# A decoder layer with routed experts: experts add straight into the output, and a branch for rare steps moves to the middle

## The chip, the cores and the metric

The kernel runs on one core of one Trainium2 chip. The metric is the device time of a whole execution in microseconds: the median of three runs, and beside it one execution that the hardware profiler recorded, with all instructions, waits and DMA packets. Engines are TensorE (PE; PEld are its weight loads), VectorE (DVE), ScalarE (ACT), GpSimd (POOL) and SyncE (SP, which only issues transfers).

## The reference

Eight rows of 256 tokens with 256 features pass three blocks with residuals: a linear attention, a cross attention to a context, and a mixture of eight experts of which each token takes its best two.

```python
x = x + _L0_attn_ref(_layernorm(x), ...)
x = x + _L0_xattn_ref(_layernorm(x), ctx_1024, ctx_1024, ...)
x = x + _L0_ffn_ref(_layernorm(x), ...)      # itself returns its input plus the experts' sum
...
combine, idx = _top2_gate(xn, Wg)
for each expert e:                            # W1[e]: 256 x 1024, W2[e]: 1024 x 256
    h = gelu(xn @ W1[e] + b1[e])
    out += gate[e] * (h @ W2[e] + b2[e])      # gate is 0 for tokens that did not choose e
```

Everything is float32.

## The kernel before

**Front.** For each of the eight rows the attention, the cross attention and the gate are computed; the loops of the rows overlap. `last_norms` writes the normed tokens to a DRAM tensor `rows_d`, `base` writes the residual part of the result to a DRAM tensor `acc` (L609). Each token's two choices get a slot each in a DRAM table `slots` (token number and gate), sorted by expert in tiles of 128; unused slots keep token numbers from NTOK = 2048 up, for which `rows_d` has rows of zeros and `acc` has spare rows.

**Expert steps.** The tokens of one tile are worked on by one expert in one step. At most NSTEP = 39 steps can be needed; how many are is known only on the chip (`total`). SURE = NSTEP - 3 = 36 steps are always run. For step s, `said` loads the expert or the tile number from a list in SBUF into a register of an engine; then

- `fetch_slots` (SP) loads token numbers and gates of the tile, `fetch_weights` (SP) the expert's first weight matrix (w1, 1 MB, three buffers, two steps ahead) and second bias (b2, three buffers);
- `gather` (POOL, indirect DMA, three steps ahead) fetches the 128 token rows, `turn` transposes them on PE, and DVE copies them out of PSUM (L889);
- `first_chunk` (L906, L910): in eight chunks PE multiplies by w1 into PSUM tiles `ph`, and ACT applies the gelu; `second_chunk` (L919) multiplies the chunks of the step before by the second matrix, which stays in SBUF, into `py`. First and second chunks of neighbouring steps alternate on PE;
- `add_out` (DVE, L934) makes yg = gate * py + bias, and `scatter` (POOL, L940) adds its rows to `acc` by an accumulating indirect DMA. Each scatter waits until the one before has landed.

`steps` is a generator with the order of all this for steps first to last; the orders of PE, ACT, DVE and SP are those of the source, and `in_turn` keeps POOL's.

**End.** After the 36 steps all five engines load `total`, and `tc.If(n_steps > SURE)` (L1212, L1216) holds the three rare steps. Behind it SP copies `acc` to the output (L1225). In the arm that is not taken each engine waits for its own last instruction (SP and POOL for their transfers) and then adds to the semaphores what the skipped instructions would have added.

Of the kernel before, what the change touches and what calls it, by code (L numbers as in the profile page):

```python
# [23 lines left out]
CLAMPED = "the list is made on the chip and clamped to this range"  # L24
# [5 lines left out]
def decoder_kernel(  # L30
# [57 lines left out]
    slots = dram.tile([NTILE, 2 * P], I32, name="slots")  # L88
    slot_rows = slots[:, :].rearrange("q (r c) -> (q r) c", c=2)
    rows_d = dram.tile([NTOK + P, D], F32, name="rows_d")  # L90
    acc = dram.tile([NTOK + P, D], F32, name="acc")

    def ps(name):
        return psum.tile([P, 512], F32, tag="ps", name=name)

    def wide(name):
        return psum.tile([P, 512], F32, tag="wide", name=name)
# [4 lines left out]
    def tokens(t, b):  # L102

        return t[S * b : S * (b + 1), :].rearrange("(s p) d -> p s d", p=P)
# [149 lines left out]
    vcols = const("vcols", [P, n_rows])  # L254
    gamma_c = vcols[:, n_b1 : n_b1 + KD]
# [596 lines left out]
    plans, ids, xgs, w1s, b2s, ready, hidden, summed = ({} for _ in range(8))  # L852

    def fetch_slots(s):
        q_sp = said(s, 1, ET.SP)
        ids[s] = mpool.tile([P, 2], I32, tag="ids", name=f"ids{s}", bufs=16)
        got = nc.sync.dma_start(ids[s], slot_rows[bass.ds(q_sp * P, P), :])
        if s in (0, NA):
            for name in puts[0 : RA * T * 2] if s == 0 else puts:
                tc.add_manual_dep(got.ins, name, WRITTEN, reason="all slots are written")  # L860

    def fetch_weights(s):
        e_sp = said(s, 0, ET.SP)
        w1s[s] = mpool.tile([P, KD, F], F32, tag="w1", name=f"w1_{s}", bufs=3)
        nc.sync.dma_start(
            w1s[s], w1_rows[bass.ds(e_sp * D, D), :].rearrange("(k p) f -> p k f", p=P)
        )
        b2s[s] = mpool.tile([P, D], F32, tag="b2", name=f"b2_{s}", bufs=3)
        nc.sync.dma_start(b2s[s], b2_flat[bass.ds(e_sp * D, D)].partition_broadcast(P))

    def reach(s):

        return RA * S if s < NA else NTOK + P
# [6 lines left out]
        ))  # L880

    def turn(s):
        p = ps(f"pt_{s}")
        xg = xgs.pop(s)
        for k in range(KD):
            nc.tensor.transpose(p[:, k * P : (k + 1) * P], xg[:, k * P : (k + 1) * P], ident)  # L886
        ready[s] = mpool.tile([P, KD, P], F32, tag="xgT", name=f"xgT{s}")
# [7 lines left out]
    CHUNKS = [c for pair in zip(range(FC // 2), range(FC // 2, FC)) for c in pair]  # L895

    def first_chunk(s, c):
        if c == CHUNKS[0]:
            hT = mpool.tile([P, FC, P], F32, tag="hT", name=f"hT{s}")
            p = [wide(f"ph_{s}_{i}").rearrange("p (c n) -> p c n", n=P) for i in range(2)]  # L900
            hidden[s] = hT, p, said(s, 0, ET.Activation)
        hT, p, e_act = hidden[s]
        half, at = divmod(c, FC // 2)
        p = p[half][:, at, :]
        for k in range(KD):
            nc.tensor.matmul(  # L906
                p, w1s[s][:, k, c * P : (c + 1) * P], ready[s][:, k, :],
                start=(k == 0), stop=(k == KD - 1),
            )
        nc.scalar.activation(  # L910
            hT[:, c, :], p, AF.Gelu_apprx_tanh,
            bias=vcols[:, bass.ds(e_act * FC + c, 1)],
        )

    def second_chunk(s, c):
        if c == CHUNKS[0]:
            summed[s] = ps(f"py_{s}"), said(s, 0, ET.PE)
        p, e_pe = summed[s]
        nc.tensor.matmul(  # L919
            p[:, 0:D], hidden[s][0][:, c, :], w2_flat[:, bass.ds((e_pe * FC + c) * D, D)],  # L920
            start=(c == CHUNKS[0]), stop=(c == CHUNKS[-1]),
        )

    def gate_of(s):
        return ids[s][:, 1:2].bitcast(F32)
# [1 line left out]
    def scale_bias(s):  # L927
        nc.scalar.activation(b2s[s], b2s[s], AF.Copy, scale=gate_of(s))  # L928

    def add_out(s):  # L930
        p, _ = summed.pop(s)
        del hidden[s]
        yg = mpool.tile([P, D], F32, tag="yg", name=f"yg{s}", bufs=3)
        nc.vector.scalar_tensor_tensor(  # L934
            yg, p[:, 0:D], gate_of(s), b2s.pop(s), op0=ALU.mult, op1=ALU.add
        )
        in_time(scatter, s, yg)

    def scatter(s, yg):
        in_turn(nc.gpsimd.indirect_dma_start(  # L940
            out=acc[0 : reach(s), :],
            out_offset=bass.IndirectOffsetOnAxis(ap=ids.pop(s)[:, 0:1], axis=0),
            in_=yg[:, :], in_offset=None, compute_op=ALU.add,
        ))

    held, holding = [], [False]
# [1 line left out]
    def in_time(what, *args):  # L948
        if holding[0]:
            held.append((what, args))  # L950
        else:
            what(*args)
# [4 lines left out]
            what(*args)  # L957
        held.clear()

    SURE = NSTEP - 3  # L960
    SLOTS, ROWS, WEIGHTS = 5, 3, 2

    def steps(first, last):


        got = max(NA, first + ROWS)
        for s in range(first, last + 1):
            if s + WEIGHTS < last and s > first:
                fetch_weights(s + WEIGHTS)
            while 6 <= s and got <= min(s + SLOTS, last - 1):  # L970
                fetch_slots(got)
                got += 1
            if s + ROWS < last:
                in_time(gather, s + ROWS)
            at = 0
            for j, c in enumerate(CHUNKS):
                took = 0.0
                if s < last:
                    first_chunk(s, c)
                    took += 0.44  # L980

                for c in CHUNKS[at : at + (2 if s == last - 1 else 1)]:
                    if s > first:
                        second_chunk(s - 1, c)
                        took += 0.43
                    at += 1
                if s > first and j == 1:
                    scale_bias(s - 1)
                if s > first and at == FC:
                    at += 1  # L990
                    add_out(s - 1)
                if j == FC - 3 and s + 1 < last:
# [5 lines left out]
            yield took  # L998

    work = steps(0, SURE)  # L1000

# [207 lines left out]
    for _ in plan:  # L1209
        pass  # L1210
    meanwhile(1e6)
    n_steps = nc.values_load(  # L1212
        total[0:1, 0:1], min_val=0, max_val=NSTEP,
        skip_runtime_bounds_check_because=CLAMPED,
    )
    with tc.If(n_steps > SURE):  # L1216
# [8 lines left out]
    nc.sync.dma_start(out.rearrange("b s d -> (b s) d"), acc[0:NTOK, :])  # L1225

# [1 line left out]
_A, _X, _F = "L0_attn_", "L0_xattn_", "L0_ffn_"  # L1228
_INS = [
# [31 lines left out]
```

## Time and profile before

| | us |
|---|---|
| median of 3 runs | 456.35 (455.56 to 458.42) |
| profiled execution | 453.33 |
| its span, first to last instruction | 451.6 |
| PE busy | 432.7 (96%) |
| ACT, DVE, POOL busy | 212.6, 186.4, 186.9 |
| scatters: time on POOL, issue to landing (median) | 1.59 each, 5.8 |
| gathers: time on POOL | 1.00 each |

The span is what the page and all answers of the trace count from; the 1.7 us between it and the execution's time lie around it. In the page's strips each digit is the busy share of one fortieth of the span in tenths (11.3 us). A wait line names who waited, for whom, the total in us, how often, and the longest. An indirect DMA's time on POOL is the making of its descriptors; its landing comes later. Rows of the trace that end in q (PEldq, SPq) are the sequencer of an engine: waits, register work, branches and DMA issues.

### The profile page before, as it was taken

Reading aid. Unit: us, or ns where it says so; the run is one execution under the profiler, and the core shown is the slowest. Engines: PE = TensorE matmul, PEld = TensorE weight load, DVE = VectorE, ACT = ScalarE, POOL = GpSimd, SP = SyncE. Lnnn points to the kernel's source line nnn. Section 1 sums busy time; section 2 is a strip of 40 time slices with the busy share of each in tenths; the row PEclk is TensorE's granted clock in tenths of the full one; section 3 lists DMA queues with packets and bytes.
Section 4 is the critical chain, followed back from the end, with each engine's and each line's share of the span. In section 5 each row is a group of like instructions: output and inputs, shape, how many; then the busy total and the mean of one; then the engine's idle time right before and its main releaser. Section 6 shows DMA issues by size and latency. Waiting matters only on the chain. (4 is left out here: it accounts for less than half of the span.)

```text
span 451.6 us, 8531 instructions
## 1 busy us (share of the span) xinstructions
PE 432.7 (96%) x2679; PEld 373.6 (83%) x2679; DVE 186.4 (41%) x692; ACT 212.6 (47%) x551; POOL 186.9 (41%) x201
## 2 busy tenths in 40 slices
PE   9999999999999999999999999999999999999960
PEld 7568777776868689999999999999999999999950
DVE  2676878687898767454111112121111212121100
ACT  3644555564555455454444444444444444444420
POOL 7314363636445662637243342424333242432220
PEclk9999999999999999999999999999999999999995
DMA  8703266755603254797776857577675766757225
GB/s 227 218 25 117 71 210 64 217 115 174 132 23 114 42 176 140 203 222 181 198 225 182 235 154 239 160 232 204 188 222 168 220 187 221 195 195 219 47 31 195
DMA packets 48369, 74.38 MB, mean 165 GB/s; under 512 B 9773, under 2 KB 37810, under 8 KB 48290
## 3 DMA queue, kind: packets, MB, share of 16 engines
q1 hardware_dynamic: 39298, 63.10, 46.3%
q0 software_dynamic: 8208, 9.91, 12.4%
q10 hardware_dynamic: 816, 0.79, 0.6%
q8 instruction: 24, 0.39, 0.4%
q14 instruction: 23, 0.19, 0.2%
HBM read 64.44 MB, written 11.44 MB: 168 GB/s over the span
## 5 line engine op out<-in xcount | busy, mean ns | idle before, releaser
L906 PEld LDWEIGHTS ph<-xgT,w 128*128 128x128 f32 x1152 | 169.5, 191 | 13.2 <-ACT hT L910 0.7
L906 PE MATMUL ph<-xgT,w 128*128 128x128 f32 x1152 | 174.8, 275 | 0.6 <-ACT hT L910 0.3
L919 PE MATMUL py<-w_s,hT 128*128 x576 | 170.3, 381 | 0.0
L910 ACT ACTIVATE hT<-ph,vcols 128x128 f32<-128x128 f32 x288 | 105.3, 367 | 137.2 <-PE ph L906 133.1
L940 POOL DMA_INDIRECT acc<-yg,ids x36 | 57.1, 1587 | 138.3 <-DMA acc<-yg,ids 75.9
L889 DVE TENSOR_SCALAR xgT<-pt,vcols 128x128 f32<-128x128 f32 x72 | 26.2, 405 | 151.9 <-PE pt L886 151.9
L919 PEld LDWEIGHTS py<-w_s,hT 128*128 128x128 f32 x576 | 88.3, 192 | 0.6
L877 POOL DMA_INDIRECT xg<-rows_d,ids x36 | 36.0, 1000 | 18.5 <-PE ph L906 10.7
L934 DVE SCALAR_TENSOR_TENSOR yg<-py,ids,b 128x256 f32<-128x256 f32 x36 | 17.4, 483 | 44.9 <-ACT hT L910 33.9
L733 POOL DMA_INDIRECT slots<-pay,posi x32 | 31.8, 993 | 9.0 <-issue 8.0
L347 PE MATMUL pxkv<-xwkv_s,cT 128*128 128x512 f32 x64 | 30.1, 593 | 0.0
L347 PE MATMUL pkv<-wkv_s,hT 128*128 128x512 f32 x64 | 29.9, 593 | 0.0
L347 PEld LDWEIGHTS pxkv<-xwkv_s,cT 128*128 128x128 f32 x64 | 11.5, 190 | 8.0 <-issue 7.7
L928 ACT ACTIVATE b<-b,ids 128x256 f32<-128x256 f32 x36 | 17.9, 498 | 0.0
L347 PEld LDWEIGHTS pkv<-wkv_s,hT 128*128 128x128 f32 x64 | 11.1, 190 | 8.2 <-issue 8.1
L309 POOL TENSOR_TENSOR rs_b<-ve_b,mhalf 128x2 f32<-128x2 f32 x8 | 8.2, 1022 | 23.1 <-DVE ve_b L322 23.1
L309 POOL TENSOR_TENSOR rs_a<-ve_a,mhalf 128x2 f32<-128x2 f32 x8 | 5.7, 708 | 26.9 <-DVE ve_a L322 25.9
L347 PEld LDWEIGHTS po<-wo_s,turnedoT 128*128 128x128 f32 x64 | 12.1, 190 | 4.6 <-issue 3.3
L511 ACT COPY turnedoT<-pto 128x512 f32<-128x512 f32 x8 | 4.7, 585 | 23.6 <-PE pto L341 23.6
L410 PE MATMUL pq<-hT,wq_s 128*128 128x256 f32 x64 | 15.2, 381 | 0.2 <-ACT hT L386 0.2
L347 PE MATMUL pfc<-xwfc_s,turnedq2T 128*128 128x256 f32 x64 | 15.2, 380 | 0.0
L347 PE MATMUL po<-wo_s,turnedoT 128*128 128x256 f32 x64 | 15.2, 380 | 0.0
(193 smaller groups left out, 523.4 us busy)
## 6 DMA issues: line engine op xcount, KB each, us to landing
w<-in_L_ffn_W_dram SPq DMA_DIRECT2D x36, 1024.0 KB, 5.4
w_s<-in_L_ffn_W_dram SPq DMA_DIRECT2D x8, 1024.0 KB, 8.6
b<-in_L_ffn_b_dram SPq DMA_DIRECT2D x36, 128.0 KB, 3.1
x<-in_x_dram SPq DMA_DIRECT2D x8, 256.0 KB, 3.5
rows_d<-h SPq DMA_DIRECT2D x8, 256.0 KB, 6.3
acc<-x SPq DMA_DIRECT2D x8, 256.0 KB, 5.2
c<-in_ctx_dram SPq DMA_DIRECT2D x7, 256.0 KB, 3.0
ids<-slots SPq DMA_DIRECT2D x36, 1.0 KB, 2.2
```

Source lines behind the costliest of these rows:

```text
L309: in_turn(nc.gpsimd.tensor_tensor(dst, src, mhalf[:, 0:n], ALU.pow))
L347: nc.tensor.matmul(p[:, 0:width], srcT[:, k, t * P : (t + 1) * P], w[:, k, 0:width], start=(k == 0), stop=(k == KD - 1),)
L410: nc.tensor.matmul(p[:, m, :], wq_s[:, k, m * P : (m + 1) * P], st["hT"][:, k, :], start=(k == 0), stop=(k == KD - 1),)
L733: ins = nc.gpsimd.indirect_dma_start(out=slot_rows, out_offset=bass.IndirectOffsetOnAxis(ap=posi[:, t, c : c + 1], axis=0), in_=pay[:, at ...
L877: in_turn(nc.gpsimd.indirect_dma_start(out=xgs[s][:, :], out_offset=None, in_=rows_d[0 : reach(s), :], in_offset=bass.IndirectOffsetOnAxis ...
L889: nc.vector.tensor_scalar(ready[s][:, k, :], p[:, k * P : (k + 1) * P], gamma_c[:, k : k + 1], beta_c[:, k : k + 1], op0=ALU.mult, op1=ALU ...
L906: nc.tensor.matmul(p, w1s[s][:, k, c * P : (c + 1) * P], ready[s][:, k, :], start=(k == 0), stop=(k == KD - 1),)
L910: nc.scalar.activation(hT[:, c, :], p, AF.Gelu_apprx_tanh, bias=vcols[:, bass.ds(e_act * FC + c, 1)],)
L919: nc.tensor.matmul(p[:, 0:D], hidden[s][0][:, c, :], w2_flat[:, bass.ds((e_pe * FC + c) * D, D)], start=(c == CHUNKS[0]), stop=(c == CHUNK ...
L928: nc.scalar.activation(b2s[s], b2s[s], AF.Copy, scale=gate_of(s))
L934: nc.vector.scalar_tensor_tensor(yg, p[:, 0:D], gate_of(s), b2s.pop(s), op0=ALU.mult, op1=ALU.add)
L940: in_turn(nc.gpsimd.indirect_dma_start(out=acc[0 : reach(s), :], out_offset=bass.IndirectOffsetOnAxis(ap=ids.pop(s)[:, 0:1], axis=0), in_= ...
```

## The change

`acc` is gone: `base` writes to the output, the scatters add into it, and the copy at the end is left out. A scatter now carries a bound: rows with a token number beyond it are dropped instead of being added to spare rows.

The branch for the three rare steps no longer stands at the end but in step FORK = SURE - 18 = 18, ahead of its seventh chunk, and has PE, DVE, ACT and SP alone. What it runs, `seldom`, uses tiles that are free by then (attention weights and the like) in place of new buffers. Its gathers are issued in steps 15 to 17 and its slot loads in steps 14 to 16, whether needed or not; its scatters are issued in any case in steps 19, 24 and 29 ahead of the fifth chunk (`late` tiles hold what they add; where the steps are not needed all their rows are beyond the bound). `ids` has 24 buffers instead of 16, `b2` four instead of three.

```diff
-    acc = dram.tile([NTOK + P, D], F32, name="acc")
+    out_rows = out.rearrange("b s d -> (b s) d")
...
-        nc.sync.dma_start(acc[NTOK:, :], zero)
...
-        nc.sync.dma_start(tokens(acc, b), x3)
+        nc.sync.dma_start(tokens(out_rows, b), x3)
...
     def fetch_weights(s):
         e_sp = said(s, 0, ET.SP)
-        w1s[s] = mpool.tile([P, KD, F], F32, tag="w1", name=f"w1_{s}", bufs=3)
...
+        b2s[s] = bo_b
+        if s < SURE:
+            w1s[s] = mpool.tile([P, KD, F], F32, tag="w1", name=f"w1_{s}", bufs=3)
+            b2s[s] = mpool.tile([P, D], F32, tag="b2", name=f"b2_{s}", bufs=4)
...
+    lent = {}
+
+    def own(kind, s, make):
+        if s < SURE:
+            return make()
+        if kind not in lent:
+            lent[kind] = make()
+        return lent[kind]
...
     def turn(s):
-        p = ps(f"pt_{s}")
+        p = own("pt", s, lambda: ps(f"pt_{s}"))
...
+    def add_out(s):
+        sum_out(s)
+        in_time(scatter, s)
+
+    def scatter(s):
         in_turn(nc.gpsimd.indirect_dma_start(
-            out=acc[0 : reach(s), :],
+            out=out_rows[0 : min(reach(s), NTOK), :],
             out_offset=bass.IndirectOffsetOnAxis(ap=ids.pop(s)[:, 0:1], axis=0),
-            in_=yg[:, :], in_offset=None, compute_op=ALU.add,
+            in_=ygs.pop(s), in_offset=None, compute_op=ALU.add,
+            bounds_check=min(reach(s), NTOK) - 1, oob_is_err=False,
         ))
...
-    SURE = NSTEP - 3
+    SURE = NSTEP - RARE
+    FORK = SURE - 18
...
+            rare = SURE + s - FORK
+            if SURE <= rare + 4 < NSTEP:
+                fetch_slots(rare + 4)
+            if SURE <= rare + 3 < NSTEP:
+                gather(rare + 3)
             at = 0
             for j, c in enumerate(CHUNKS):
+                if s == FORK and j == 6:
+                    seldom()
+                rare, behind_fork = divmod(s - FORK - 1, 5)
+                if j == 4 and 0 <= rare < RARE and behind_fork == 0:
+                    scatter(SURE + rare)
...
+    def seldom():
+        n_steps = nc.values_load(
+            total[0:1, 0:1], engines=[ET.PE, ET.DVE, ET.Activation, ET.SP],
+            min_val=0, max_val=NSTEP, skip_runtime_bounds_check_because=CLAMPED,
+        )
+        with tc.If(n_steps > SURE):
+            for s in range(SURE, NSTEP):
+                ygs[s] = late[s - SURE]
+            for s in range(SURE, NSTEP):
+                fetch_weights(s)
+                turn(s)
+                scale_bias(s)
+                for c in CHUNKS:
+                    first_chunk(s, c)
+                for c in CHUNKS:
+                    second_chunk(s, c)
+                sum_out(s)
...
-    n_steps = nc.values_load(
-        total[0:1, 0:1], min_val=0, max_val=NSTEP,
-        skip_runtime_bounds_check_because=CLAMPED,
-    )
-    with tc.If(n_steps > SURE):
-        for s in range(SURE, NSTEP):
-            fetch_slots(s)
-            fetch_weights(s)
-        for s in range(SURE, NSTEP):
-            gather(s)
-        turn(SURE)
-        for _ in steps(SURE, NSTEP):
-            pass
-    nc.sync.dma_start(out.rearrange("b s d -> (b s) d"), acc[0:NTOK, :])
```

More of the change, by code (lines that the diff above doesn't have):

```diff
@@ L851, in decoder_kernel @@
     done = []
-    plans, ids, xgs, w1s, b2s, ready, hidden, summed = ({} for _ in range(8))
+    plans, ids, xgs, w1s, b2s, ready, hidden, summed, ygs = ({} for _ in range(9))
     def fetch_slots(s):
         q_sp = said(s, 1, ET.SP)
-        ids[s] = mpool.tile([P, 2], I32, tag="ids", name=f"ids{s}", bufs=16)
+        ids[s] = mpool.tile([P, 2], I32, tag="ids", name=f"ids{s}", bufs=24)
         got = nc.sync.dma_start(ids[s], slot_rows[bass.ds(q_sp * P, P), :])
@@ L863, in fetch_weights, with first_weights @@
         e_sp = said(s, 0, ET.SP)
-        w1s[s] = mpool.tile([P, KD, F], F32, tag="w1", name=f"w1_{s}", bufs=3)
-        nc.sync.dma_start(
-            w1s[s], w1_rows[bass.ds(e_sp * D, D), :].rearrange("(k p) f -> p k f", p=P)
-        )
-        b2s[s] = mpool.tile([P, D], F32, tag="b2", name=f"b2_{s}", bufs=3)
-        nc.sync.dma_start(b2s[s], b2_flat[bass.ds(e_sp * D, D)].partition_broadcast(P))
+        b2s[s] = bo_b
+        if s < SURE:
+            w1s[s] = mpool.tile([P, KD, F], F32, tag="w1", name=f"w1_{s}", bufs=3)
+            b2s[s] = mpool.tile([P, D], F32, tag="b2", name=f"b2_{s}", bufs=4)
+        w = w1_rows[bass.ds(e_sp * D, D), :].rearrange("(k p) f -> p k f", p=P)
+        if s < SURE:
+            nc.sync.dma_start(w1s[s], w)
+        else:
+            w1s[s] = wkv_s, xwkv_s
+            for i, half in enumerate(w1s[s]):
+                at = i * (F // 2)
+                nc.sync.dma_start(half[:, :, 0 : F // 2], w[:, :, at : at + F // 2])
+        nc.sync.dma_start(b2s[s], b2_flat[bass.ds(e_sp * D, D)].partition_broadcast(P))
+    def first_weights(s, k, c):
+        if s < SURE:
+            return w1s[s][:, k, c * P : (c + 1) * P]
+        half, at = divmod(c, FC // 2)
+        return w1s[s][half][:, k, at * P : (at + 1) * P]
+    lent = {}
+    def own(kind, s, make):
+        if s < SURE:
+            return make()
+        if kind not in lent:
+            lent[kind] = make()
+        return lent[kind]
     def reach(s):
@@ L886, in turn @@
             nc.tensor.transpose(p[:, k * P : (k + 1) * P], xg[:, k * P : (k + 1) * P], ident)
-        ready[s] = mpool.tile([P, KD, P], F32, tag="xgT", name=f"xgT{s}")
+        ready[s] = bv_b.rearrange("p (k q) -> p k q", k=KD)
+        if s < SURE:
+            ready[s] = mpool.tile([P, KD, P], F32, tag="xgT", name=f"xgT{s}")
         for k in range(KD):
@@ L895, in decoder_kernel, with hidden_tiles @@
     CHUNKS = [c for pair in zip(range(FC // 2), range(FC // 2, FC)) for c in pair]
+    def hidden_tiles(s):
+        if s < SURE:
+            hT = mpool.tile([P, FC, P], F32, tag="hT", name=f"hT{s}")
+            return [hT[:, c, :] for c in range(FC)]
+        pair = [ft("x", f"hT{s}{i}", [P, FC // 2, P], bufs=4) for i in range(2)]
+        return [pair[c // (FC // 2)][:, c % (FC // 2), :] for c in range(FC)]
     def first_chunk(s, c):
         if c == CHUNKS[0]:
-            hT = mpool.tile([P, FC, P], F32, tag="hT", name=f"hT{s}")
-            p = [wide(f"ph_{s}_{i}").rearrange("p (c n) -> p c n", n=P) for i in range(2)]
+            hT = own("hT", s, lambda: hidden_tiles(s))
+            p = own("ph", s, lambda: [
+                wide(f"ph_{s}_{i}").rearrange("p (c n) -> p c n", n=P) for i in range(2)
+            ])
             hidden[s] = hT, p, said(s, 0, ET.Activation)
@@ L906, in first_chunk @@
             nc.tensor.matmul(
-                p, w1s[s][:, k, c * P : (c + 1) * P], ready[s][:, k, :],
+                p, first_weights(s, k, c), ready[s][:, k, :],
                 start=(k == 0), stop=(k == KD - 1),
@@ L910, in first_chunk @@
         nc.scalar.activation(
-            hT[:, c, :], p, AF.Gelu_apprx_tanh,
+            hT[c], p, AF.Gelu_apprx_tanh,
             bias=vcols[:, bass.ds(e_act * FC + c, 1)],
@@ L916, in second_chunk @@
         if c == CHUNKS[0]:
-            summed[s] = ps(f"py_{s}"), said(s, 0, ET.PE)
+            summed[s] = own("py", s, lambda: ps(f"py_{s}")), said(s, 0, ET.PE)
         p, e_pe = summed[s]
         nc.tensor.matmul(
-            p[:, 0:D], hidden[s][0][:, c, :], w2_flat[:, bass.ds((e_pe * FC + c) * D, D)],
+            p[:, 0:D], hidden[s][0][c], w2_flat[:, bass.ds((e_pe * FC + c) * D, D)],
             start=(c == CHUNKS[0]), stop=(c == CHUNKS[-1]),
@@ L928, in scale_bias, with sum_out @@
         nc.scalar.activation(b2s[s], b2s[s], AF.Copy, scale=gate_of(s))
-    def add_out(s):
+    RARE = 3
+    late = [w[:, k, 0:D] for w in (wo_s, xwq_s) for k in range(KD)]
+    def sum_out(s):
         p, _ = summed.pop(s)
         del hidden[s]
-        yg = mpool.tile([P, D], F32, tag="yg", name=f"yg{s}", bufs=3)
+        ygs[s] = late[s - SURE] if s >= SURE else mpool.tile(
+            [P, D], F32, tag="yg", name=f"yg{s}", bufs=3
+        )
         nc.vector.scalar_tensor_tensor(
-            yg, p[:, 0:D], gate_of(s), b2s.pop(s), op0=ALU.mult, op1=ALU.add
+            ygs[s], p[:, 0:D], gate_of(s), b2s.pop(s), op0=ALU.mult, op1=ALU.add
         )
-        in_time(scatter, s, yg)
-    def scatter(s, yg):
+    def add_out(s):
+        sum_out(s)
+        in_time(scatter, s)
+    def scatter(s):
         in_turn(nc.gpsimd.indirect_dma_start(
-            out=acc[0 : reach(s), :],
+            out=out_rows[0 : min(reach(s), NTOK), :],
             out_offset=bass.IndirectOffsetOnAxis(ap=ids.pop(s)[:, 0:1], axis=0),
-            in_=yg[:, :], in_offset=None, compute_op=ALU.add,
+            in_=ygs.pop(s), in_offset=None, compute_op=ALU.add,
+            bounds_check=min(reach(s), NTOK) - 1, oob_is_err=False,
         ))
@@ L998, in steps @@
             yield took
+    def seldom():
+        n_steps = nc.values_load(
+            total[0:1, 0:1], engines=[ET.PE, ET.DVE, ET.Activation, ET.SP],
+            min_val=0, max_val=NSTEP, skip_runtime_bounds_check_because=CLAMPED,
+        )
+        with tc.If(n_steps > SURE):
[10 more added lines that the diff above has]
+                sum_out(s)
     work = steps(0, SURE)
@@ L1211, in decoder_kernel @@
     meanwhile(1e6)
-    n_steps = nc.values_load(
-        total[0:1, 0:1], min_val=0, max_val=NSTEP,
-        skip_runtime_bounds_check_because=CLAMPED,
-    )
-    with tc.If(n_steps > SURE):
-        for s in range(SURE, NSTEP):
-            fetch_slots(s)
-            fetch_weights(s)
-        for s in range(SURE, NSTEP):
-            gather(s)
-        turn(SURE)
-        for _ in steps(SURE, NSTEP):
-            pass
-    nc.sync.dma_start(out.rearrange("b s d -> (b s) d"), acc[0:NTOK, :])
 _A, _X, _F = "L0_attn_", "L0_xattn_", "L0_ffn_"
```

## The prediction

> **What bounds the kernel now.** I read the span in forty slices, then the timeline of the last fifteen microseconds, then busy time by stretch.
>
> ```profile
> PE   9999999999999999999999999999999999999960
> ...
> PEclk9999999999999999999999999999999999999995
> ```
>
> TensorE is the bound to within two slices of the end. Busy time by stretch (per engine: us and count; then granted clock, DMA share, GB/s):
>
> ```profile
> core 0: us, PE busy (x) PEld busy (x) DVE busy (x) ACT busy (x) POOL busy (x), PEclk, DMA share, GB/s
> 300.00:360.00 60.00, 60.00 (x417) 56.17 (x416) 10.42 (x26) 27.39 (x74) 20.61 (x16) 1.00 0.69 201
> ...
> 436.90:441.60 4.70, 0.00 (x0) 0.00 (x0) 0.48 (x1) 0.00 (x0) 1.55 (x1) 0.87 0.28 31
> 441.60:451.60 10.00, 0.00 (x0) 0.00 (x0) 0.00 (x0) 0.00 (x0) 0.00 (x0) 0.50 0.57 211
> ```
>
> In the expert steps PE is busy 60.00 of 60.00 us; one step is 7.25 us (the yg instructions on DVE stand at 302.88 and 310.12). Nothing off PE can gain time there. The tail is different (start, us, engine, what, idle time before it and who ended that):
>
> ```profile
> 435.79 1.03 PE L919 MATMUL py<-w_s,hT 128*128 x4
> ...
> 436.91 0.48 DVE L934 SCALAR_TENSOR_TENSOR yg<-py,ids,b 128x256 f32<-128x256 f32 x1 [4.75 <-PE py L919]
> 437.67 1.55 POOL L940 DMA_INDIRECT acc<-yg,ids  x1 [3.69 <-DVE yg L934]
> 441.56 0.61 SPq L1225 DMA_DIRECT2D out_dram<-acc  x1
> ```
>
> PE ends at 435.79 + 1.03 = 436.82. The last scatter goes at 437.67, lands 3.8 us later (the median that the DMA view gives for this stretch), and only then SP starts the copy of acc to the output, which lands after 8.3 us. From PE's end to the span's end are 14.8 us in which no engine computes anything but that one sum.
>
> **The copy goes: a gain.** Without acc, the base rows and the scatters write the output itself, so L1225 and its wait vanish. What stays after the last landing (SP goes on at 441.56) is the program's end. SP's trace there shows one semaphore instruction each 0.06 us: six of them and two drains took 0.43 us after the copy landed (449.85 to 450.28), and the closing barrier 1.28 us (450.28 to 451.56). Now up to ten waits are left behind the last scatter, 0.6 us. New end: 441.56 + 0.6 + 1.28 = 443.4, 8.2 us before the old one. A 128 KB write of zeros into acc (L252, at 16.2 us, DMA alone) goes too, worth nothing under a full PE.
>
> **The branch moves into step 18: a loss on PE.** Before, the branch at the end cost nothing: PE's and ACT's lay under the tail, SP's 20 us earlier. Its rows (minimum/median/maximum ns):
>
> ```profile
> L1216 ACTq COMPARE_BRANCH  x1: 45/45/45, 433.8 to 433.8; - x1
> L1216 PEldq COMPARE_BRANCH  x1: 3477/3477/3477, 434.5 to 434.5; - x1
> L1216 DVEq COMPARE_BRANCH  x1: 72/72/72, 437.6 to 437.6; - x1
> ...
> L1216 POOLq INC_SWDGE_SEM  x1: 1584/1584/1584, 438.5 to 438.5; - x1
> ```
>
> Now PE, DVE, ACT and SP each load the step count and jump over three steps of code after chunk 5 of step 18, and in the other arm each waits for all it has issued and adds the skipped counts. On PE, matmuls of the old trace at this place lie end to end; its sequencer issues the two transposes of step 19 about 1.6 us before PE has run them (the register work ahead of the next chunk's matmul leads it by 1.1 to 1.35 us). The load is 0.31 us and the branch begins some 1.2 us before PE runs dry. The rows for a taken branch are far apart: on ACT 45 ns, and the next instruction 0.33 us after its start; on PE 3.48 us. In that stall queue q8, 24 packets and 0.39 MB on the page, so 16 KB each, made a fetch at 435.67 out of its rhythm of about 17 us. PE runs 110 instructions a step (50 loads, 50 matmuls, 10 others), hence 256 per fetch at 64 bytes: q8 is PE's code, and the jump of some 332 instructions (three steps) left what was loaded. Laying a grid of 16.9 us (256 / 110 x 7.25) under the fetches, the old branch stands some 213 instructions into a block and its target, at 545, in the block after the next. The new one stands some 72 into its block (4.7 us behind the border); its target, at 404, is in the next, which is fetched 0.7 to 5.9 us after a border. So I take the short branch: 0.35 us, hidden by the 1.2 us lead; then PE must be dry (the arm waits for its last matmul), and two semaphore instructions at 0.15 us each (438.07, 438.22, 438.37 in the old trace), a dispatch and a weight load (190 ns) follow: 0.7 us of standstill. With the long branch: 3.48 - 1.2 + 0.5 = 2.8 us.
>
> The Trainium skill, "Runtime: NRT & Kernel Launch", section Instruction fetch mechanics, says that a taken branch whose target is outside the current two pages forces a fetch before execution goes on; by that rule alone, with 16 KB pages, a 332-instruction jump may go either way, and the sum is 0.7 or 2.8 us. The old trace agrees with the rule for the far target; no run shows the near one.
>
> The spare steps take PSUM buffers in turn (four of each tag), so py of step 18 now gets py of step 17's buffer and must await its yg: it would start one chunk of ph (0.44 us) after py 17 ends, but yg ends 0.09 + 0.48 us after and is seen some 0.15 us later: 0.3 us more. Fork in sum: 1.0 us (0.4 to 3.1).
>
> The others are covered. ACT's sequencer is free from 307.77, 0.11 us behind the start of a gelu, until the next gelu at 308.75, and needs 0.29 + 0.33 + 0.16. DVE loads (0.54 us) behind the second xgT copy that ends at 309.04, and its yg is due at 310.12. SP must wait for all its transfers, w1 of step 20 among them (5.4 us to landing), and next is asked for w1 of step 21 when step 18 is over; b2 with four buffers no longer holds SP until yg (b2 at 310.63, behind yg at 310.12), so w1 is issued up to 3 us earlier in each step and the wait is over before. An ACT or DVE fetch of the 3.48 us sort would cost 1.4 to 2.4 us; their jumps are 58 and 15 instructions, and 45 and 72 ns speak against it.
>
> **Three gathers and three scatters in any case, on POOL.** A gather is 0.99 us on POOL, a scatter 1.59, with three more slot loads on SP. POOL is busy 20.6 of 60 us, but waits:
>
> ```profile
> POOL acc L940 <- DMA acc<-yg,ids: 75.9, 18, 5.5
> ```
>
> Each scatter waits for the one before to land: 5.8 us median, plus 0.74 us to the next start, against a step of 7.25. From 247 to 355 us the fifteen scatters follow each other at 7.2 us: this queue is all but full. An added scatter, in steps 19, 24 and 29, has only rows beyond the bound; dropped rows are in no row of this trace, so its landing lies between POOL's 1.6 us and a full scatter's 8.1. I take 3.8, the quiet landing, since nothing has to be moved. The queue then runs 4.5 us late. Late ones land sooner: started 1.5 us after yg they took 6.4 to 7.6 us (268.31, 289.90, 347.84), 2.7 us after it 5.2 to 5.4 (276.70, 341.70), 4.3 us after it 4.3 (234.72). So a late queue gains 1 to 2 us a step and has five steps each time; the last two steps are shorter (5.6 and 5.2 us) but land in 3.8. Gathers are three steps ahead, yg has three buffers: nothing on PE waits. Cost 0, and if the cover fails, see below. The check against the bound on every scatter: between 0 and, say, the 0.6 us by which a scatter exceeds a gather; 0 taken, since it counts once, at the tail.
>
> **Sum.** Profiled execution 453.33 us, span 451.6: -8.2 + 1.0 = -7.2, so 446.1 with a span of 444.4. The median of the runs, 456.35, stands 3.0 above that execution; I carry the difference over: 449.2 us.
>
> **Rivals.**
> PE's far fetch (chance 0.20): the next block is not yet in, or the count of instructions is off. For it the 3.48 us row, against it the near target. 449.2 + 2.1 = 451.3. The pause of 2.8 us stays below the 3.5 us after which the clock halves in the tail (x + 0.5(4.7 - x) = 0.87 x 4.7). The Trainium skill, "TensorE: Matmul & The Clock Gate", Part 1, puts that window at about 3.4 us; the trace agrees with its 3.5.
> POOL's closing drain (0.14):
>
> ```profile
> L1257 POOLq DRAIN  x3: 46/252/6012, 440.1 to 451.3; - x3
> ```
>
> Its 6.01 us ended at 446.08 and lay under the copy. It stood behind the semaphore instruction of 1.58 us that POOL no longer has, which speaks for 0.3 us now; if it belongs to the scatter, the end is 439.3 + 6.0 + 1.24 = 446.6 instead of 443.4: 452.4. With the far fetch as well (0.05): 454.5.
> Slower (0.13): the scatter queue does not drain. From when an average link (landing + 0.74) over steps 19 to 33 exceeds about 6.1 us, 3 x 6.5 = 19.5 us of added links outlast the slack of 15 x (7.25 - link) and of the last two steps (5.4 - 4.55 each, 1.7), and the last scatter is late by the rest: at today's 7.2 by 19.5 - 0.7 - 1.7 = 17, 449.2 + 17 = 466. The 7.2 speaks for it, the short landings of late scatters and of those after 355 us (3.9 to 4.3) against.
> That the spare steps run after all: the old trace has 36 scatters, not 39, on the same inputs; no chance given.
>
> **Numbers.** Forecast 0.48 at 449.2 (its own range 447.7 to 450.5). 1%, about what a measurement of this kernel tells from no change, is 4.6 us: the far fetch at 451.3 is mostly faster still. Faster 0.48 + 0.14 = 0.62; within 1% the drain, both together and the rest of the far fetch, 0.25; slower 0.13. The range, 447.7 to 454.5, leaves out the queue and a little below.
>
> **What would show it.** No copy and a span end 2 us after the last landing; a gap on PE in step 18 of 0.7 us (or 2.8, with PE's COMPARE_BRANCH over 1 us); steps of 7.25 us on both sides; the last scatter 0.85 us after PE's end and not later; POOL's drain ending within 0.3 us of the landing. A scatter starting late at the end, or PE gaps after 19, 24 and 29, would make me wrong.

## The result, and the profile after

| | before | after |
|---|---|---|
| median of 4 runs each, us | 456.98 (455.56 to 458.42) | 450.77 (448.01 to 452.00) |
| profiled execution, us | 453.33 | 452.00 |
| its span, us | 451.6 | 450.3 |
| last matmul ends, us of the span | 436.82 | 444.30 |
| from there to the span's end, us | 14.7 | 6.0 |

The ratio is 0.989 (95% interval 0.9846 to 0.9934; the two medians alone give 0.986): faster by a little over 1%. The forecast was 449.2 with a range of 447.7 to 454.5. The two profiled executions differ by 1.3 us and the medians by 6.2, because the one of before was faster than all four of its runs and the one of after the slowest of its four; the changed kernel is therefore profiled a second time below. The medians of the runs below leave out executions more than 1.5% above the fastest of their kernel (one of ten in a2 and in e6, three of ten in e12).

The span in forty slices, after:

```profile
PE   9899999999999998999999999998999998999994
...
PEclk9999999999999999999999999999999999999999
```

PE now falls below 9 in slices 2, 16, 28 and 34 (11.3 us each) and in the last one; before, only at the end. Slice 28, from 304 to 315 us, holds the fork (the step with the branch), slice 34, from 371 to 383, a wait for gathered rows, slice 16 a late copy on ACT at 170, which costs PE 1.4 us. Slice 2 costs nothing: ahead of slice 16 PE is still 0.1 us earlier than before. A late gelu on ACT at 219 us costs another 1.2. Busy time by stretch (per engine: us and count; then granted clock, DMA share, GB/s):

```profile
core 0: us, PE busy (x) PEld busy (x) DVE busy (x) ACT busy (x) POOL busy (x), PEclk, DMA share, GB/s
300.00:360.00 60.00, 57.90 (x400) 54.02 (x399) 9.70 (x24) 26.38 (x73) 21.34 (x18) 1.00 0.62 187
360.00:420.00 60.00, 57.69 (x398) 53.46 (x397) 9.70 (x24) 26.31 (x71) 23.56 (x18) 1.00 0.64 188
...
444.30:450.30 6.00, 0.00 (x0) 0.00 (x0) 0.49 (x1) 0.00 (x0) 1.55 (x1) 0.86 0.08 8
```

Before, PE was busy 60.00 of 60 us; now 2.1 us are missing in the first stretch and 2.3 in the second. The tail moves next to nothing (8 GB/s where the copy had 211). PE's waits from 300 to 430 us (who, for whom: us, times, longest) name the 4.4 us:

```profile
PE pt L908 <- DMA xg<-rows_d,ids: 2.3, 2, 1.4
PE ph L940 <- PEq L1062: 2.1, 1, 2.1
```

L1062 is the branch. Its rows (ns minimum/median/maximum):

```profile
L1062 SPq COMPARE_BRANCH  x1: 45/45/45, 307.4 to 307.4; - x1
L1062 PEldq COMPARE_BRANCH  x1: 3056/3056/3056, 309.4 to 309.4; - x1
L1062 ACTq COMPARE_BRANCH  x1: 45/45/45, 310.4 to 310.4; - x1
L1062 DVEq COMPARE_BRANCH  x1: 72/72/72, 311.4 to 311.4; - x1
```

PE's branch is the long one of 3.06 us. Queue q8, which carries PE's code, made no fetch between 290.2 and 310.1 us. The fetch that began at 310.11 ended at 311.04, and the branch ended 1.42 us after that.

The waits for xg (the gathered rows) begin on POOL. Its timeline behind the fork (start, us, what, idle time before and what ended it):

```profile
315.63 1.59 POOL L983 DMA_INDIRECT out_dram<-yg,ids  x1 [6.67 <-DVE yg L974]
317.52 0.98 POOL L899 DMA_INDIRECT xg<-rows_d,ids  x1 [0.30 <-issue]
320.93 1.59 POOL L983 DMA_INDIRECT out_dram<-wo_s,ids  x1 [2.43 <-DMA out_dram<-yg,ids]
327.99 1.56 POOL L983 DMA_INDIRECT out_dram<-yg,ids  x1 [5.47 <-DVE xgT L913]
...
335.91 1.58 POOL L983 DMA_INDIRECT out_dram<-yg,ids  x1 [5.05 <-DVE xgT L913]
```

From about 240 us to 315.63 each scatter starts 0.76 us after the instruction that makes its yg has started (all such distances below are from there). The first added one (from wo_s) lands in 6.25 us, and the next real one starts 5.9 us after its yg. Two of the rows shown put the wait down to xgT, a copy long done: what really ended it is the landing of the scatter ahead (the one of 320.93 lands at 327.18, 0.8 us before the start at 327.99). From there the queue stays 5.9 to 6.8 us late for five steps, and after the second and third added scatters 12.5. The gather behind the scatter at 370.88 is issued at 372.74, some 12 us late as well, and PE stands still in steps 27 and 32.

The tail, after, by the timeline:

```profile
441.76 2.54 PE L953 MATMUL py<-w_s,hT 128*128 x11
...
444.39 0.49 DVE L974 SCALAR_TENSOR_TENSOR yg<-py,ids,b 128x256 f32<-128x256 f32 x1 [5.10 <-PE py L953]
445.16 1.55 POOL L983 DMA_INDIRECT out_dram<-yg,ids  x1 [3.38 <-DVE yg L974]
```

and POOL's closing drain there:

```profile
L1317 POOLq DRAIN  x3: 46/103/4363, 444.9 to 450.0; - x3
```

The last scatter is on time, lands 3.7 us later at 448.8, and the drain (444.93 to 449.29) ends 0.46 us after that.

### The profile page after: what moved, and what is told of

Same layout as the page of the kernel before. It is cut to its first block, busy times and chain, and to the rows that moved or that the text cites. A ratio compares the mean times of both kernels' runs of the same rounds, so it can differ in the third digit from the quotient of the medians.

```text
span 450.3 us, 8577 instructions
## 1 busy us (share of the span) xinstructions
PE 433.1 (96%) x2679; PEld 372.3 (83%) x2679; DVE 186.5 (41%) x692; ACT 212.6 (47%) x551; POOL 195.0 (43%) x207
## 5 line engine op out<-in xcount | busy, mean ns | idle before, releaser
L983 POOL DMA_INDIRECT out_dram<-yg,ids x36 | 57.1, 1586 | 126.5 <-DVE yg L974 51.4
L899 POOL DMA_INDIRECT xg<-rows_d,ids x39 | 39.2, 1006 | 17.9 <-PE ph L940 9.8
L908 PE MATMUL pt<-ident,xg 128*128 128x128 f32 x72 | 13.9, 274 | 2.3 <-DMA xg<-rows_d,ids 2.3
```

What stands on the lines that cost most here:

```text
L899: in_turn(nc.gpsimd.indirect_dma_start(out=xgs[s][:, :], out_offset=None, in_=rows_d[0 : reach(s), :], in_offset=bass.IndirectOffsetOnAxis ...
L983: in_turn(nc.gpsimd.indirect_dma_start(out=out_rows[0 : min(reach(s), NTOK), :], out_offset=bass.IndirectOffsetOnAxis(ap=ids.pop(s)[:, 0:1 ...
```

## Experiments

Shifts are those of PE's matmuls against the profiled execution of before: where a shift grows, PE has lost that much. What the fork costs is read from the shift across it, and is the same as the length of that step, from yg to yg, less 7.25 us: 2.33 us in the profile above, where step 18 took 9.58. "Fetch" is a packet of 16 KB on q8. Ratios are to executions of the kernel before on the same chip.

### The copy alone, and the three parts of the loss

**e1.** In the kernel of before, only:

```diff
-            out=acc[0 : reach(s), :],
+            out=out_rows[0 : min(reach(s), NTOK), :],
+            bounds_check=min(reach(s), NTOK) - 1, oob_is_err=False,
...
-    nc.sync.dma_start(out.rearrange("b s d -> (b s) d"), acc[0:NTOK, :])
```

> The kernel before with only the copy taken away: base and scatters go into the output with the bound, the branch stays at the end on all five engines. Theory (the copy's chain alone was the tail): the span ends about 2 us after the last scatter has landed, PE's end stays near 436.8 us of the span, and the time falls by 8.2 us. Rival (POOL's closing drain): POOL's drain of 6.0 us, which in the kernel before stood behind a semaphore instruction of 1.6 us, starts at 440.1 as before, ends 4.5 us after the landing, and the time falls by only some 4 us.

448.49 us median, ratio 0.988 (0.985 to 0.991). PE ends at 436.82 again; the bounded scatter takes 1.55 us on POOL as before (last one), so the check is free. But the span ends at 446.8: the rival.

```profile
L1256 POOLq DRAIN  x3: 46/103/5844, 440.1 to 446.5; - x3
```

The drain ends at 445.9, 4.6 us after the last landing. Without the copy over it, it is the tail: 9.9 us from PE's end instead of the 6.0 of the changed kernel.

**e2.** In the changed kernel, the three added scatters left out:

```diff
-                if j == 4 and 0 <= rare < RARE and behind_fork == 0:
-                    scatter(SURE + rare)
```

> The changed kernel without the three added scatters (their rows all lie beyond the bound here, so the output loses nothing on these inputs; with more steps it would lack the rare experts' sums). Theory (they put POOL's queue late, and with it the gathers): every scatter starts about 0.8 us after its yg through to the end, PE's two waits for gathered rows in steps 27 and 32 (1.61 and 1.14 us) are gone, and PE's end comes 2.75 us earlier. Rival (the queue is full by itself, and would be late without them): the scatters drift late all the same, and the waits stay.

449.32 us median, ratio 0.992 (0.989 to 0.995). The theory holds for the queue: from 240 us on every scatter starts 0.76 us after its yg (one 0.95), and PE's only wait from 255 to 440 us is one of 0.4 us at the fork. The kernel gained little all the same, since its drain became long:

```profile
L1315 POOLq DRAIN  x3: 46/103/8462, 437.4 to 446.4; - x3
```

It ends 8.2 us after the start of the last scatter, where the changed kernel has 4.1. And, not expected: PE's branch, at the very same place in PE's code, is short here.

```profile
L1060 PEldq COMPARE_BRANCH  x1: 463/463/463, 306.2 to 306.2; - x1
```

There was a fetch at 301.5, ahead of the branch. The fork cost 0.59 us.

**e3.** Only one rare step behind the branch:

```diff
-            for s in range(SURE, NSTEP):
+            for s in range(SURE, SURE + 1):
                 fetch_weights(s)
```

> The changed kernel with only the first of the three rare steps behind the branch (the second and third rare step are left out), so PE jumps over some 110 instructions instead of 332. Theory (the branch costs PE 3.06 us because its target is in a block of code not yet loaded): the target is now in the same block, PE's branch takes about 0.35 us, the gap on PE in step 18 is some 0.7 instead of 2.26 us, and PE's end comes about 1.6 us earlier. Rival (a taken branch on PE costs some 3 us wherever it leads): the branch takes 3 us again and nothing changes.

448.23 us median, ratio 0.988 (0.985 to 0.992).

```profile
L1062 PEldq COMPARE_BRANCH  x1: 237/237/237, 306.6 to 306.6; - x1
```

As the theory had it: 0.24 us, and 0.53 us lost at the fork, although q8 had made no fetch from 287.2 to 307.25, when the branch was over. A target in the block at hand, as it is by the prediction's count, needed none. One wait for xg stays (1.03 us), and the last scatter starts 2.0 us after its yg.

**e4.** No branch at all:

```diff
-        n_steps = nc.values_load(
...
-        with tc.If(n_steps > SURE):
...
+        for s in range(SURE, NSTEP):
+            ygs[s] = late[s - SURE]
```

> The changed kernel without load, branch and rare steps (the rare steps are left out; their scatters stay). It prices the whole fork: step 18 should take 7.25 us again instead of 9.58, so PE's end comes 2.3 us earlier, with the two waits for gathered rows in steps 27 and 32 as they were or up to 2.3 us longer in sum, if the queue of scatters gained from the pause. Rival (the wait for a buffer of py in step 18 is a cost of its own): about 0.3 us of step 18 stay.

446.99 us median, ratio 0.983 (0.978 to 0.987). PE loses nothing at all in step 18. That does not test the rival: the PSUM buffers that the rare steps take, which would make py wait, are left out with them. The changed kernel's own profile does: from the second matmul behind the branch on its shift stays at 4.74 us until the first wait for xg, so py cost nothing. Here a wait for xg costs 1.53 us, and the last scatter starts 1.8 us after its yg.

### Both kernels once more

**a2**, the changed kernel:

> The changed kernel once more, unaltered. Theory (PE's branch is short or long according to whether its next block of code has been fetched by then, which falls anywhere in some 6 us; ACT's two late starts at 170 and 219 us were accidents of one execution): the same instructions give another fork, either a branch of about 0.3 to 0.5 us and a shift of 0.6 us, or 3 us and 2.4 us again, and the two late starts (+1.46 and +0.98 us) are gone; the two waits for gathered rows stay, 1.5 to 2.8 us in sum. Rival (all of it belongs to the program): +1.46, +0.98, +2.36, +1.62 and +1.14 us at the same places again.

450.02 us median, ratio 0.988 (0.985 to 0.990). The fork is much the same: a branch of 3.28 us, no fetch from 288.3 to 308.2, 2.56 us lost. So the long branch came in both profiles of this program; e2's short one has one profile, so that chance has no part in it is not shown. One wait for xg of 1.11 us is left of two. ACT's late start at 170 us is there again (PE loses 1.3 us), that at 219 is not.

**b2**, the kernel before:

> The kernel before, unaltered, once more. Theory (the late start of ACT's copy at 170 us, 1.4 us on PE, belongs to the execution or the chip and not to the change): it shows here too wherever the kernels beside it show it. Rival (the change brings it): it is absent here and present in the kernels beside it.

455.93 us in one execution. It shows no loss at 170 us, but neither did the kernels beside it (they lost 1.3 to 1.8 us at 212 us, which it did not). The loss at 170 is in both profiles of the changed kernel and in the three variants that ran on the chip of the second, but not in the variants that ran on three other chips; whether the change has a part in it stays open.

### Where the late queue reaches PE

**e5.** Gathers one step further ahead:

```diff
-        xgs[s] = mpool.tile([P, D], F32, tag="xg", name=f"xg{s}", bufs=6)
+        xgs[s] = mpool.tile([P, D], F32, tag="xg", name=f"xg{s}", bufs=7)
...
-    SLOTS, ROWS, WEIGHTS = 5, 3, 2
+    SLOTS, ROWS, WEIGHTS = 6, 3, 2
...
-            if s + ROWS < last:
+            if s + ROWS < last and s <= FORK - 6:
                 in_time(gather, s + ROWS)
+            if s + ROWS + 1 < last and s >= FORK - 6:
+                in_time(gather, s + ROWS + 1)
```

> The changed kernel with gathers four steps ahead from step 12 on (seven buffers of xg). Theory (the late queue of scatters reaches PE only through the gathers behind it): PE's waits for gathered rows vanish, 1.5 to 2.8 us; but PE no longer gives the queue these pauses, so the last scatter starts 2 to 4 us after its yg instead of 0.8 to 2.0, and of the gain on PE at most 1 us is left at the span's end. Rival (the scatters catch up in the shorter last steps anyway): the last scatter is on time and the whole 1.5 to 2.8 us is gained.

447.44 us median, ratio 0.981 (0.976 to 0.987), on the chip of the second run of the changed kernel. The waits for xg are gone, as the theory said; the only one left on PE is the fork:

```profile
PE ph L940 <- PEq L1064: 2.0, 1, 2.0
```

The other half of the theory fell: the queue is late by 6 to 12.6 us in between, but the last scatter starts 0.76 us after its yg. Of the versions that compute everything this has the lowest ratio, 0.6% under the changed kernel's, with intervals that just overlap.

### What makes PE's branch long

**e6.** Fork five chunks later (step 19, ahead of its fourth chunk), gathers as in the changed kernel:

```diff
-    FORK = SURE - 18
+    FORK = SURE - 17
...
-                if s == FORK and j == 6:
+                if s == FORK and j == 3:
```

> The changed kernel with the fork five chunks later (step 19, ahead of chunk 3), some 70 of PE's instructions deeper into its block of code, so that the next block should have come in. Theory (block not yet loaded): PE's branch takes 0.5 us or less, and the shift on PE at the fork is 0.4 to 0.6 us. Rival (chance in every run, wherever the branch stands in its block): 3 us at about the same rate as at the old place. The added scatters come one step later too, so the last scatter may start some 1 to 2 us later after its yg.

453.30 us median, ratio 0.995 (0.991 to 0.998). A fetch came at 303.2, the branch at 312.7 took 0.38 us and the fork cost 0.53. But 2.1 us after PE had gone on it stood again (busy time by stretch):

```profile
312.00:314.00 2.00, 1.80 (x13) 1.35 (x11) 0.00 (x0) 1.21 (x4) 1.67 (x2) 1.00 0.72 289
314.00:318.00 4.00, 2.10 (x13) 1.76 (x13) 0.00 (x0) 0.73 (x2) 0.94 (x1) 1.00 0.72 203
318.00:321.50 3.50, 3.38 (x13) 2.92 (x14) 0.73 (x2) 0.74 (x2) 0.00 (x0) 0.58 0.00 0
```

By the prediction's count the target lies some 30 to 40 instructions ahead of the next border, and the next fetch came only at 315.8. It ended at 316.8 and PE went on 1.3 us after that; PE lost 2.15 us, and then 1.7 more, with a granted clock of 0.58 in that stretch.

**e9.** Fork six steps and three chunks earlier, in the kernel of e5:

```diff
-    FORK = SURE - 18
+    FORK = SURE - 24
...
-                if s == FORK and j == 6:
+                if s == FORK and j == 3:
```

> Fork in step 12 ahead of chunk 3 (seven steps, 770 of PE's instructions or three blocks of code, ahead of the fork five chunks later), added scatters in steps 13, 18 and 23, gathers four steps ahead. Theory (the queue needs time behind the last added scatter, and PE must not wait for gathers meanwhile): no wait for gathered rows, the last scatter 0.76 us after its yg, a fork of 0.4 to 0.6 us; PE ends within 1 us of the kernel before. POOL's closing drain tells two theories apart: with 110 indirect DMAs as in the changed kernel it ends 0.5 us after the last landing if their number decides (110 so far gave 0.46 us, 104 and 107 gave 4.6), and the time is about 9 us under the kernel before; if a queue that is late to the end decides, it ends 4.6 us after the landing, and the time is 5 us under it.

450.31 us median, ratio 0.987 (0.982 to 0.992). Queue and drain did what was expected: the last scatters on time, no wait for xg, the drain's end 0.47 us after the landing. PE did not: a branch of 0.45 us, 0.54 us lost at it, then 2.55 us until 1.3 us after the next fetch had ended, and 1.7 at half clock, as in e6.

**e12.** In the kernel of e5, the load of w1 in step 18 is put behind the branch:

```diff
-            if s + WEIGHTS < last and s > first:
+            if s + WEIGHTS < last and s > first and s != FORK:
                 fetch_weights(s + WEIGHTS)
...
                     seldom()
+                    fetch_weights(s + WEIGHTS)
```

> Gathers four steps ahead as before, and in step 18 alone the next load of w1 is issued behind the branch instead of at the step's start. Theory (the fetch of PE's next block of code waits behind a load of w1: with three added scatters left out it started at 301.48, 0.27 us ahead of the issue of w1; in the changed kernel nothing came until the burst of w1 at 306.4 to 310.0 was over): with no load in the way the fetch comes some 0.7 us behind the border, PE's branch takes 0.5 us or less and the shift at the fork is 0.4 to 0.6 instead of 2.1 to 2.4 us, so the time falls by some 1.7 us against the same kernel with the load in front (ratio 0.981 to the kernel before), to about 0.978. Rival (the fetch is late by the program's own layout, whatever the DMA queues carry): 3 us again, and nothing gained.

450.65 us median, ratio 0.990 (0.985 to 0.994). The edit missed: SP runs ahead of PE, took its branch at 300.7 and issued that load at 304.4 as ever. The branch took 3.45 us, the fork 2.7, and 1.5 went at half clock. It decides nothing on the load.

**e13.** The same with a true wait, for the first gelu behind the fork:

```diff
+            if behind is not None:
+                tc.add_manual_dep(got.ins, behind, WRITTEN, reason="behind the fork")
...
+                    gelu = first_chunk(s, c)
+                    if s == FORK and j == 6:
+                        fetch_weights(s + WEIGHTS, gelu.ins.name)
```

> Gathers four steps ahead as before, and the load of w1 for step 20 now truly waits for the first gelu behind the fork in step 18 (order alone had left it at 304.4 us). Theory (the fetch of PE's next block of code, asked for at the border some 5 us ahead of the branch, waits behind the load of w1 that is issued 0.8 us after the border): no load is issued between 297 and 310 us, the fetch starts between 303.5 and 306 us, PE's branch takes 0.5 us or less, and the shift on PE at the fork is 0.4 to 0.6 instead of 2.1 to 2.75 us. The load then lands some 5.5 us after 311, 2 us ahead of step 20; if that fails, a wait for w shows there. Rival (the fetch is made only when PE asks for the target, or at a place in the code that these programs pass too late, whatever the DMA queues carry): no fetch until the branch, which takes 2.9 us or more, and a shift of 2.1 us or more.

445.86 us median, ratio 0.985 (0.982 to 0.989). The load went at 311.1, and no packet of w1 moved from 301.6 to 312.1. Still the fetch came at 307.1 only:

```profile
L1068 PEldq COMPARE_BRANCH  x1: 2907/2907/2907, 306.8 to 306.8; - x1
```

So here the fetch was as late with no load under way; the rival stands. What the traces do show is that the branch waits for this fetch: in all six profiles with a long branch in the middle (the changed kernel twice, e5, e11, e12, e13) the fetch begins 0.3 to 1.1 us after the branch and the branch ends 1.40 to 1.42 us after the fetch; the branch at the end in the three profiles with the old place ends 1.40 to 1.43 us after its fetch. In e3 a fetch comes 0.7 us after the branch too, though that branch had no need of it.

The queue of scatters tells something else here. It is 4.7 to 8.2 us late from 228 to 303 us, before any added scatter, and catches up where the load is held back: the scatters at 302.36 and 306.97 land in 3.8 and 3.1 us, after 6.0 to 7.9 for all but one of those from 228 to 295. Behind the added scatters it is late again, to the end: the last scatter starts 3.2 us after its yg, and from PE's end to the span's end are 8.5 us.

The profiled execution also shows the clock fall behind the pause:

```profile
307.66 0.38 PE L910 MATMUL pt<-ident,xg 128*128 128x128 f32 x2
310.00 0.68 PE L942 MATMUL ph<-xgT,w 128*128 128x128 f32 x4 [1.96 <-PEq L1068]
310.52 0.79 PE L955 MATMUL py<-w_s,hT 128*128 x2
311.10 1.06 PE L942 MATMUL ph<-xgT,w 128*128 128x128 f32 x4
...
314.36 0.61 PE L942 MATMUL ph<-xgT,w 128*128 128x128 f32 x4
```

Four matmuls that take 0.61 us take 1.06 until 314.4: 1.7 us lost.

### What ends POOL's drain

**e11.** In the changed kernel, the three added scatters replaced by three gathers of the same rows:

```diff
-                    scatter(SURE + rare)
+                    in_turn(nc.gpsimd.indirect_dma_start(
+                        out=late[rare], out_offset=None, in_=rows_d[0 : reach(s), :],
...
```

> The changed kernel with three gathers of zero rows into unused tiles in place of the three added scatters (which add nothing on these inputs): 110 indirect DMAs again, but the queue of scatters is on time. Theory (the number of indirect DMAs decides how long POOL's closing drain lasts): it ends 0.5 us after the last landing, 4.1 us after the start of the last scatter, and the span ends 6 us after PE. Rival (added scatters, not added DMAs, shorten it): 8.2 us after the start of the last scatter, span 9.9 us after PE, as without them. Either way every scatter starts 0.76 us after its yg and no wait for gathered rows is over 0.2 us.

448.86 us in one execution.

```profile
L1322 POOLq DRAIN  x3: 46/103/4439, 441.7 to 446.9; - x3
```

The drain ends 4.2 us after the last scatter's start, though the queue was on time throughout: three more indirect DMAs of either kind do it. All ten profiles with 110 of them have 3.9 to 4.2 us, the four with 104 or 107 have 8.2 to 9.0. What in the number decides (a threshold, a remainder) was not tried.

## Why the prediction was right, and where it was not

| us against the span of before | predicted | after | again |
|---|---|---|---|
| tail | -8.2 | -8.74 | -8.95 |
| fork | +1.0 | +2.33 | +2.56 |
| waits for gathers | 0 | +2.75 | +1.11 |
| other shifts on PE, ahead of the fork | 0 | +2.40 | +0.69 |
| sum | -7.2 | -1.26 | -4.59 |

(The first three rows are read from the tail and the shifts; the fourth is the rest of PE's shift at its end, 7.48 and 4.36 us.) The median fell by 6.2 us, close to the forecast's 7.2, though the terms came out otherwise; the rows show less than the medians because the profiled execution of before, which they compare with, was 3.7 us under its median. Against the second profile of the kernel before (b2: span 454.2, tail 15.4) a2's span is 7.2 us shorter. So the nearness of 449.2 to 450.77 owes something to luck: a tail that fell for another reason than the one given, and executions of the kernel before that differ among themselves by 3 us and more.

**The tail** was right in place and, within 0.8 us, in size: no copy, the span's end 1.5 us after the landing, the drain's 0.46 after it (the prediction said within 0.3). Its reason was wrong. The prediction let POOL's drain fall to 0.3 us since the semaphore instruction of 1.58 us ahead of it goes. e2 has no such instruction and a drain of 8.46 us. The rival "POOL's closing drain" had the drain right, and its end of 446.6 is e1's (446.8) and e2's (446.7); it failed in the changed kernel only because the added scatters made 110 indirect DMAs. They paid for 4 us of the gain that the prediction credited to the copy alone.

**The fork** is the term that was mis-sized: 1.0 us taken, 2.33 and 2.56 measured. The failed step is "its target, at 404, is in the next, which is fetched 0.7 to 5.9 us after a border. So I take the short branch". With the branch 4.7 us behind the border that was no certainty, and this program's fetch had not come by then; the far-fetch rival (2.8 us, 451.3) is what happened. Where the target was in (e3) or the next block had come (e2, e6, e9) the fork cost 0.53 to 0.59 us: the short price of 0.7 was sound, and the 0.3 us for py on top of it did not come. The Trainium skill, "Runtime: NRT & Kernel Launch", section Instruction fetch mechanics, has a target outside the two current pages fetched before execution goes on; by that rule a target in the next block goes either way, as that block is in or not, and e2 and the changed kernel, with the same PE code up to the branch, show the two cases. Why the block was in by then in the one and not in the other stays open.

**The pause and the clock.** "The pause of 2.8 us stays below the 3.5 us after which the clock halves" held in both profiles of the changed kernel but not in general: e6, e9, e12 and e13 ran at half clock behind pauses of 1.9 to 2.5 us (PE's wait in each), for 1.5 to 1.7 us of loss, while the changed kernel (2.1, 2.3), e5 (2.0) and e11 (1.8) did not. The length of the pause does not decide; the clock's records in the traces show what goes with it. Every stretch at half clock there is 3.41 us long, and every change of the clock, in all the profiles, lies a whole number of 3.41 us after the clock's first change to full. PE's busy time in the windows of this grid, in e13 (half clock from 310.79 to 314.20):

```profile
307.37:310.79 3.42, 1.46 (x11) 1.13 (x10) 0.73 (x2) 0.44 (x2) 2.20 (x2) 1.00 0.26 54
310.79:314.20 3.41, 3.41 (x14) 3.05 (x13) 0.48 (x1) 0.88 (x3) 0.32 (x1) 0.50 0.68 198
```

in e11, which kept its clock:

```profile
309.54:312.95 3.41, 1.62 (x12) 1.31 (x12) 0.73 (x2) 0.37 (x1) 0.00 (x0) 1.00 0.24 57
```

and in the changed kernel, whose pause fell across an edge of the grid:

```profile
308.63:312.04 3.41, 2.05 (x15) 1.65 (x13) 0.73 (x2) 0.78 (x3) 0.33 (x1) 1.00 0.44 130
312.04:315.45 3.41, 2.68 (x18) 2.58 (x19) 0.48 (x1) 0.86 (x3) 0.00 (x0) 1.00 0.09 10
```

In all eight profiles with such a pause the clock halved in the next window where PE was busy for 1.50 us or less of one (e6 1.50, e9 1.47, e13 1.46, e12 1.28), and did not where it was busy for 1.62 or more. One window elsewhere does not fit (b2, at 16 us, where the clock halved behind 2.0 us of work). The Trainium skill, "TensorE: Matmul & The Clock Gate", Part 1, says that the window of about 3.4 us is free-running and does not reset when the kernel starts. The traces agree with both: 3.41 us, and a first change to full that comes anywhere from 4.6 to 7.0 us after the span's start, so that the edges fall at another place of the program in each execution.

**The queue** was the other wrong term: cost 0, by "A late queue gains 1 to 2 us a step" and "Gathers are three steps ahead, yg has three buffers: nothing on PE waits". A scatter without a row to move was taken to land in 3.8 us; it took 5.6 to 6.3 in the first profile and 3.9 to 6.8 in the second. And a late queue did not gain: what goes with the landing time is not lateness but the place against the load of w1, which is issued now 0.5 us ahead of each yg. Over all profiles of variants with loads at that place, scatters that start 0.8 us or 2.2 to 5.4 us after their yg mostly land in 3.6 to 6.1 us; those at 5.5 to 7.4 us, just around the next load, mostly in 5.7 to 7.5, as long as loads go on. The kernel before has it with the lateness alike: at 397.85 and 405.10 a scatter starts 0.76 us after its yg, but the next load comes 1.59 us later in the one and 0.67 in the other, and they land in 4.08 and 7.25 us. And e13 caught up where a load was held back. With 0.74 us to the next start a landing of 6 to 7 us is one step each, so the queue stays there. e2 and e5 show the two halves of the chain: without added scatters no lateness from 240 us on; with gathers issued a step earlier lateness, but no loss on PE. e13 shows that an added scatter is not the only way into that place. The slower rival (queue does not drain to the end, 466) did not come: the last steps have no loads, and the queue caught up, in the changed kernel in time for the last scatter. In e3, e4 and e13 the last scatter was still 1.8 to 3.2 us behind its yg, where 0.76 is on time.

**The other covers** held: ACT's and DVE's branches took 45 and 72 ns, the bound nothing that shows, steps apart from the named places are 7.25 us.

## What to carry to other kernels

When work that hides something is removed, price what lay under it: here a drain of 6 us stood under the copy, and it was luck that the change also shortened it. A branch on an engine that never rests costs what its code fetch costs, and both the target and what has to be fetched behind the target have to be looked at. A pause costs more when it fills most of one window of the clock than when it falls across an edge. A serial queue that is all but full should be given slack where it feeds the bounding engine (gathers a step earlier) before anything is added to it.

## What was not expected of the hardware

- The closing drain on POOL ends 0.45 to 0.47 us after the last landing in the ten profiles with 110 indirect DMAs in the program, and 4.6 to 4.7 us after it in the four with 104 or 107.
- A scatter whose rows are all beyond the bound lands no sooner than a full one: in 5.0 to 6.9 us in 25 of 27 cases, in 3.9 and 2.7 in the other two.
- A branch on PE whose target is not in ends 1.40 to 1.43 us after the fetch of 16 KB does, in nine profiles of nine.
- PE's code fetches repeat at the same instruction in both profiles of the changed kernel (within some 20 instructions), yet a program with the same PE code up to the branch (e2) makes the one in question some 70 instructions ahead of it. In e13 it was late with no load of w1 under way; what decides stays open.
- Pauses of 1.8 to 2.5 us on PE halved its clock for 3.41 us in four of eight profiles: in those where PE was busy for 1.50 us or less of one window of the clock's fixed grid of 3.41 us.
